# Layer 1's banded attention in blocks of 64 keys and 96 queries, on 64x64 tiles of TensorE

## The chip, the core and the metric

The kernel runs on one core of a Trainium2 chip. The metric is the device time of one execution in microseconds (us); lower is better. PE is the matmul engine (TensorE), PEld its weight loads, DVE the vector engine, ACT the scalar engine, POOL the general one, SP the queue that issues most DMAs. SBUF is the on-chip memory that all engines read; PSUM holds matmul results, in eight banks of 512 f32 numbers for each of 128 partitions.

## What is computed

x has 128 rows of 256 positions with 256 channels. Two layers follow each other, each `x + attention(groupnorm(x))`, with attention among the 256 positions of one row. Layer 0 has eight heads of 32 channels, a bias from pairs and a gate. Layer 1, which the change is about, has four heads of 64 channels and a band:

```python
q, k, v = jnp.split(x2 @ w_in.T + b_in, 3, axis=-1)      # four heads of 64
scores = jnp.einsum('bhid,bhjd->bhij', q, k) / sqrt(64)
keep = jnp.abs(i - j) <= 16                               # 256 queries i, 256 keys j
attn = softmax(jnp.where(keep, scores, -inf), axis=-1)
out = jnp.einsum('bhij,bhjd->bhid', attn, v)
y = out @ w_out.T + b_out
```

All data and all matmuls are f32.

## The kernel before, in words

An early stage transposes weights, takes statistics of x and computes layer 0's pair bias. A loop over rows does layer 0 and stores x1 to memory, a second one does layer 1, and a last block, entered only if a softmax sum was out of bounds, repeats all with a shifted softmax.

Layer 1's loop runs over s, the row. Each row has these parts, on PE unless another engine is named:

- `piece(s, 0)`: four transposes into `px` (L222), and two DVE operations (L227) that normalise it into `xn`.
- `piece(s, 1)` and `piece(s, 2)`: the q and k projections `p1q`, `p1k` (L239), channel by position; ACT adds the bias and writes `1q`, `1k` (L430), two operations each.
- `piece(s, 3)`: the v projection `p1v` (L250), position by channel in two halves of 128 positions; DVE adds the bias and writes `1v` (L435).
- `scores(s)`: for each head and each of two blocks of 128 keys one matmul over the 144 queries that the band can reach (L445), with keys as output partitions and 64 channels as rows, into one bank `1sim` per head. ACT takes Exp of each into `1ex` (L453), POOL multiplies by the 0/1 mask `seen` into `1p` (L455).
- `attend(s)`: v times p into `1av`, and a matrix of ones times p into `1zs`, the softmax sums (L472), each 64 output partitions by 144 queries. ACT copies the sums to `1z` and adds them up (L479); DVE takes the reciprocal `1rz` (L481), multiplies into `1at` (L483), and keeps the smallest sum in `zmin` (L485).
- `finish(s)`: the output projection `1po` (L250); DVE adds its bias into `1o` (L495), POOL adds x1 (L496), and every four rows SP stores them (L498).

`px`, `p1q`, `p1k`, `p1v` and `1po` share two PSUM banks, the pool `ps_proj` (tag `proj`); `1sim` has four banks, and the pool `ps_av` two, one for `1av` and one for `1zs`. Each of the five keeps its bank until the engine that reads it is done. The loop is written as:

```python
for s in range(S + 1):
    if s < S: scores(s)
    piece(s + 1, 1); piece(s + 1, 2); piece(s + 1, 3)
    piece(s + 2, 0)
    finish(s - 1)
    if s < S: attend(s)
```

The order on each engine is not exactly the written one. Tile, the framework, orders the instructions when the kernel is built: among those whose inputs and buffers it reckons ready, the one written first goes first. On the chip each engine then works in that fixed order, and waits on semaphores.

Of the kernel before, what the change touches and what calls it, by code (L numbers as in the profile page):

```python
# [9 lines left out]
F32 = mybir.dt.float32  # L10
# [5 lines left out]
P = 128  # L16
# [4 lines left out]
H0, D0 = 8, 32  # L21
H1, D1 = 4, 64
BAND = 16
KQ = P + BAND
QLO = (0, R - KQ)
NEG = -3.0e38
EPS = 1e-5
Z_LOW, Z_HIGH = 1e-12, 1e15
# [3 lines left out]
def conv_preact_kernel(  # L32
# [19 lines left out]
    dram = ctx.enter_context(tc.tile_pool(name="dram", bufs=1, space=bass.MemoryType.DRAM))  # L52
    ps_proj = ctx.enter_context(tc.tile_pool(name="ps_proj", bufs=2, space=PSUM))
    ps_sim = ctx.enter_context(tc.tile_pool(name="ps_sim", bufs=4, space=PSUM))
    ps_av = ctx.enter_context(tc.tile_pool(name="ps_av", bufs=1, space=PSUM))

    def proj_bank(name):
        return ps_proj.tile([P, 2, R], F32, tag="proj", name=name)

    def sim_bank(name):  # L60
        return ps_sim.tile([P, 2, R], F32, tag="sim", name=name)
# [19 lines left out]
    bqk = const.tile([P, 4], F32, name="bqk")  # L81
    with nc.allow_non_contiguous_dma(reason="512 biases, once"):
        nc.scalar.dma_start(out=bqk, in_=b_in[0 : 2 * C].rearrange("(t p) -> p t", p=P))
    bv = const.tile([P, C], F32, name="bv")
    nc.scalar.dma_start(out=bv, in_=b_in[2 * C : 3 * C].partition_broadcast(P))
    bo = const.tile([P, C], F32, name="bo")
    nc.scalar.dma_start(out=bo, in_=b_out.partition_broadcast(P))

# [4 lines left out]
        )  # L93


    seen = const.tile([P, 2, KQ], F32, name="seen")
    nc.gpsimd.memset(seen, 1.0)
    for kt in range(2):
        d = kt * P - QLO[kt]
        keep(seen[:, kt, :], KQ, 0.0, BAND + d, 1, -1)  # L100
        keep(seen[:, kt, :], KQ, 0.0, BAND - d, -1, 1)

    w_in_t = const.tile([P, 2, 3 * C], F32, name="w_in_t")
    w_out_t = const.tile([P, 2, C], F32, name="w_out_t")
# [49 lines left out]


    with ExitStack() as early:
        xs_pool = early.enter_context(tc.tile_pool(name="xs", bufs=2))
        pr_pool = early.enter_context(tc.tile_pool(name="pr", bufs=2))
        st_pool = early.enter_context(tc.tile_pool(name="st", bufs=1))
# [106 lines left out]
    with ExitStack() as lay:  # L266
        st1 = lay.enter_context(tc.tile_pool(name="st1", bufs=1))
        stats1 = st1.tile([P, G, S // SG, 6], F32, name="stats1")
        with ExitStack() as lay0:
            big = lay0.enter_context(tc.tile_pool(name="big0", bufs=2))  # L270
            row = lay0.enter_context(tc.tile_pool(name="row0", bufs=2))
            att = lay0.enter_context(tc.tile_pool(name="att0", bufs=2))
# [129 lines left out]
        mean1, rstd1 = group_columns(st1, stats1, 1)  # L402


    with ExitStack() as lay:
        big = lay.enter_context(tc.tile_pool(name="big1", bufs=3))
        row = lay.enter_context(tc.tile_pool(name="row1", bufs=2))
        att = lay.enter_context(tc.tile_pool(name="att1", bufs=2))
        st, hd, xgs, outs = {}, {}, {}, {}

        def load(g):
            if g * XG < S:
                xg = big.tile([P, XG, 2, C], F32, tag="xg", name=f"yg{g}")
                nc.sync.dma_start(out=xg, in_=rows(x1, g * XG, XG))
                xgs[g] = xg

        def piece(s, n):
            if s >= S:
                return
            if n == 0:  # L420
                if s % XG == 0:
                    load(s // XG + 1)
                st[s] = {"xn": normalized(row, xgs[s // XG][:, s % XG], mean1, rstd1, f"1_{s}")}
            elif n in (1, 2):
                w = "qk"[n - 1]
                ps = by_channel(w_in_t, (n - 1) * C, st[s]["xn"], f"p1{w}{s}")
                a = row.tile([P, 2, R], F32, tag=w, name=f"1{w}{s}")
                for half in range(2):
                    b = bqk[:, 2 * (n - 1) + half : 2 * (n - 1) + half + 1]
                    nc.scalar.activation(a[:, half, :], ps[:, half, :], AF.Identity, bias=b)  # L430
                st[s][w] = a
            else:
                ps = by_token(st[s]["xn"], w_in_t, 2 * C, f"p1v{s}")
                v = row.tile([P, 2, C], F32, tag="v", name=f"1v{s}")
                nc.vector.tensor_tensor(v, ps, bv.unsqueeze(1).to_broadcast([P, 2, C]), ALU.add)  # L435
                st[s]["v"] = v

        def scores(s):
            q, k = st[s]["q"], st[s]["k"]
            sims = [sim_bank(f"1sim{s}_{h}") for h in range(H1)]  # L440
            for half in range(2):
                for kt in range(2):
                    for j in range(2):
                        p0 = D1 * j
                        nc.tensor.matmul(  # L445
                            sims[2 * half + j][:, kt, 0:KQ],
                            lhsT=k[p0 : p0 + D1, half, kt * P : (kt + 1) * P],
                            rhs=q[p0 : p0 + D1, half, QLO[kt] : QLO[kt] + KQ],
                            start=True, stop=True,
                        )  # L450
            ex = att.tile([P, H1, 2, KQ], F32, tag="ex", name=f"1ex{s}")
            for h in range(H1):
                nc.scalar.activation(ex[:, h], sims[h][:, :, 0:KQ], AF.Exp, scale=1.0 / math.sqrt(D1))  # L453
            p = att.tile([P, H1, 2 * KQ], F32, tag="p", name=f"1p{s}")
            nc.gpsimd.tensor_tensor(  # L455
                p, ex.rearrange("p h k q -> p h (k q)"),
                seen.rearrange("p k q -> p (k q)").unsqueeze(1).to_broadcast([P, H1, 2 * KQ]), ALU.mult,
            )
            hd[s] = p

        def attend(s):
            p, v = hd.pop(s), st[s]["v"]
            av = ps_av.tile([P, 2, R], F32, tag="avz", name=f"1av{s}")
            zs = ps_av.tile([P, 2, R], F32, tag="bv0", name=f"1zs{s}")
            for to in (av, zs):
                for half in range(2):
                    for kt in range(2):
                        for j in range(2):
                            h = 2 * half + j
                            w = v[:, kt, h * D1 : (h + 1) * D1] if to is av else ones  # L470

                            nc.tensor.matmul(  # L472
                                to[D1 * j : D1 * (j + 1), half, QLO[kt] : QLO[kt] + KQ],
                                lhsT=w, rhs=p[:, h, kt * KQ : (kt + 1) * KQ],
                                start=(kt == 0), stop=(kt == 1), skip_group_check=True,
                            )
            z = att.tile([P, 2, R], F32, tag="z", name=f"1z{s}")
            n = 2 * S + s
            nc.scalar.activation(z, zs, AF.Identity, accum_out=zsum[:, n : n + 1])  # L479
            rz = att.tile([P, 2, R], F32, tag="rz", name=f"1rz{s}")  # L480
            nc.vector.reciprocal(rz, z)  # L481
            at = row.tile([P, 2, R], F32, tag="at", name=f"1at{s}")
            nc.vector.tensor_tensor(at, av, rz, ALU.mult)  # L483
            st[s]["at"] = at
            nc.vector.tensor_reduce(zmin[:, n : n + 1], z, axis=AX.XY, op=ALU.min)  # L485

        def finish(s):
            if s < 0:
                return
            po = by_token(st[s]["at"], w_out_t, 0, f"1po{s}")  # L490
            g, k = divmod(s, XG)
            if k == 0:
                outs[g] = big.tile([P, XG, 2, C], F32, tag="o", name=f"1o{g}", bufs=2)
            o = outs[g]
            nc.vector.tensor_tensor(o[:, k], po, bo.unsqueeze(1).to_broadcast([P, 2, C]), ALU.add)  # L495
            nc.gpsimd.tensor_tensor(o[:, k], o[:, k], xgs[g][:, k], ALU.add)  # L496
            if k == XG - 1:
                nc.sync.dma_start(out=rows(out[0], g * XG, XG), in_=o)  # L498
                outs.pop(g)
            st.pop(s)  # L500

        load(0)
        for n in range(4):
            piece(0, n)
        piece(1, 0)
        for s in range(S + 1):
            if s < S:
                scores(s)
            piece(s + 1, 1)
            piece(s + 1, 2)  # L510
            piece(s + 1, 3)
            piece(s + 2, 0)
            finish(s - 1)
            if s < S:
                attend(s)


    low = const.tile([P, 1], F32, name="low")
# [10 lines left out]
    sure = nc.values_load(n_fine[0:1, 0:1])  # L529
    with tc.If(sure < P):  # L530
        with ExitStack() as lay:
            one = lay.enter_context(tc.tile_pool(name="one2", bufs=1))
            two = lay.enter_context(tc.tile_pool(name="two2", bufs=2))
            mask = one.tile([P, 2, R], F32, name="mask2")
            nc.gpsimd.memset(mask, 0.0)
            for t in range(2):
                keep(mask[:, t, :], R, NEG, BAND + t * P, 1, -1)
                keep(mask[:, t, :], R, NEG, BAND - t * P, -1, 1)
            stats2 = one.tile([P, G, NX, 6], F32, name="stats2")

            def shifted(sim, t2, name):
# [55 lines left out]
            def again(layer, s, src, dst, mean, rstd):  # L597
# [16 lines left out]
                if layer == 0:  # L614
                    nc.vector.tensor_copy(v, ps)
                else:
                    nc.vector.tensor_tensor(v, ps, bv.unsqueeze(1).to_broadcast([P, 2, C]), ALU.add)
                at = two.tile([P, 2, R], F32, tag="at2", name=f"at2_{layer}")
                attention(layer, a["q"], a["k"], v, at)
                if layer == 0:  # L620
# [45 lines left out]
```

## Time and profile before

| what | value |
|---|---|
| median of 3 runs | 3971.83 us (3971.67 to 3971.9) |
| the profiled execution | 3971.9 us, span 3970.1 us |
| PE busy | 3877.4 us, 98% of the span |
| DVE busy | 2457.1 us, 62% |
| ACT busy | 1487.1 us, 37% |
| POOL busy | 501.2 us, 13% |
| mean granted PE clock | 0.951 |

The span runs from the first instruction to the last. Busy shares are averages over the early stage (cold clock, DMA), layer 0 (to about 2425 us) and layer 1 (from about 2480 us), so what a change in layer 1 is worth has to be read from that stretch. In the timeline a line gives the start, the time taken, the engine, the source line, the operation, output and inputs, the shape, and the number of instructions merged into it; square brackets hold the idle time of the engine before it and what ended that.

### The profile page before, as it was taken

The numbers are of one execution on the slowest core, as the hardware profiler recorded it, in microseconds if no ns is written. First come the engines' busy times: TensorE is split into PE (matmuls) and PEld (weight loads), VectorE is DVE, ScalarE is ACT, GpSimd is POOL, SyncE is SP. The second block draws the span as 40 slices with busy tenths as digits, with TensorE's granted clock in tenths as the row PEclk, the third lists the DMA queues.
The fourth block names the chain that finished last, engine by engine and source line by source line (L and its number), as shares of the span: only waits on it lengthen the run. The fifth ranks groups of instructions, "written<-read, shape, count | busy, mean of one in ns | idle before, by whom it ended". The sixth has DMA issues, their size and how long they took to land. (4 is left out here: it accounts for less than half of the span.)

```text
span 3970.1 us, 75105 instructions
## 1 busy us (share of the span) xinstructions
PE 3877.4 (98%) x32294; PEld 3057.5 (77%) x32294; DVE 2457.1 (62%) x4181; ACT 1487.1 (37%) x3485; POOL 501.2 (13%) x270
## 2 busy tenths in 40 slices
PE   7999999999999999999999997999999999999998
PEld 7998777777777777777777774788888888888887
DVE  5402677767776777677766777456556555555655
ACT  2223444444444444444444442333333333333332
POOL 0000000000000000000000000233333333333333
PEclk6556999999999999999999998999999999999999
DMA  9631011101110111001110100111111111111111
GB/s 360 217 106 54 12 44 33 44 12 44 33 44 12 44 35 42 26 30 44 33 41 15 44 23 22 54 43 43 53 55 43 43 43 43 60 48 43 43 43 33
DMA packets 153826, 208.83 MB, mean 53 GB/s; under 512 B 2960, under 2 KB 135824, under 8 KB 152464
## 3 DMA queue, kind: packets, MB, share of 16 engines
q1 hardware_dynamic: 150656, 201.34, 15.8%
q8 instruction: 256, 4.19, 0.4%
q10 hardware_dynamic: 2832, 2.63, 0.2%
q14 instruction: 82, 0.67, 0.1%
HBM read 136.85 MB, written 67.11 MB: 51 GB/s over the span
## 5 line engine op out<-in xcount | busy, mean ns | idle before, releaser
L455 POOL TENSOR_TENSOR 1p<-1ex,seen 128x1152 f32<-128x1152 f32 x128 | 336.0, 2625 | 2758.9 <-ACT 1ex L453 2758.9
L481 DVE RECIPROCAL 1rz<-1z 128x512 f32<-128x512 f32 x128 | 429.2, 3353 | 246.9 <-ACT 1z L479 246.9
L318 ACT ACTIVATE ex<-sim 128x512 f32<-128x512 f32 x1024 | 528.7, 602 | 129.0 <-PE sim L311 129.0
L360 DVE RECIPROCAL d<-d 128x256 f32<-128x256 f32 x256 | 445.9, 1742 | 0.0
L356 DVE TENSOR_TENSOR t<-bv,z 128x256 f32<-128x256 f32 x256 | 108.1, 422 | 460.2 <-ACT z L354 460.2
L354 ACT ACTIVATE z<-avz 128x256 f32<-128x256 f32 x256 | 98.3, 384 | 750.4 <-PE avz L349 739.2
L479 ACT ACTIVATE 1z<-1zs 128x512 f32<-128x512 f32 x128 | 76.4, 597 | 729.0 <-issue 719.8
L321 DVE TENSOR_TENSOR both<-ex 128x512 f32<-128x512 f32 x512 | 329.1, 683 | 2.9 <-ACT ex L318 2.9
L311 PE MATMUL sim<-q,k 32*128 32x256 f32 x4096 | 293.3, 400 | 0.0
L336 PE MATMUL avz<-ex,v 128*32 128x256 f32 x4096 | 275.6, 386 | 10.5 <-DVE t L357 10.5
L343 PE MATMUL bv<-bias_sb,v 128*32 128x256 f32 x4096 | 269.6, 379 | 1.1 <-DVE t L356 1.1
L311 PEld LDWEIGHTS sim<-q,k 32*128 32x128 f32 x4096 | 184.9, 184 | 110.5 <-issue 104.9
L227 DVE TENSOR_SCALAR xn<-px,mean,rstd 128x256 f32<-128x256 f32 x512 | 253.8, 537 | 23.8 <-PE px L222 21.3
L250 PE MATMUL 1po<-w_out_t,1at 128*128 128x256 f32 x1024 | 256.9, 394 | 0.8 <-DVE 1at L483 0.8
L239 PE MATMUL p1q<-xn,w_in_t 128*128 128x256 f32 x1024 | 257.0, 394 | 0.6 <-DVE xn L227 0.6
L239 PE MATMUL pq<-xn,qkv_sb 128*128 128x256 f32 x1024 | 256.7, 394 | 0.8 <-DVE xn L227 0.7
L250 PE MATMUL pv<-qkv_sb,xn 128*128 128x256 f32 x1024 | 255.1, 392 | 0.0
L250 PE MATMUL po<-out_sb,at 128*128 128x256 f32 x1024 | 247.5, 382 | 6.5 <-DVE at L363 4.9
L496 POOL TENSOR_TENSOR 1o<-1o,yg 128x512 f32<-128x512 f32 x128 | 162.9, 1273 | 701.8 <-DVE 1o L495 699.2
L239 PE MATMUL p1k<-xn,w_in_t 128*128 128x256 f32 x1024 | 242.4, 380 | 0.0
L239 PE MATMUL pg<-xn,gate_sb 128*128 128x256 f32 x1024 | 241.9, 379 | 0.0
L250 PE MATMUL p1v<-w_in_t,xn 128*128 128x256 f32 x1024 | 241.9, 379 | 0.0
(91 smaller groups left out, 6314.6 us busy)
## 6 DMA issues: line engine op xcount, KB each, us to landing
xs<-in_x_dram SPq DMA_DIRECT2D x8, 4096.0 KB, 22.1
xg<-in_x_dram SPq DMA_DIRECT2D x32, 1024.0 KB, 7.5
x<-o SPq DMA_DIRECT2D x16, 2048.0 KB, 8.4
yg<-x SPq DMA_DIRECT2D x32, 1024.0 KB, 8.1
out_dram<-1o SPq DMA_DIRECT2D x32, 1024.0 KB, 5.3
qkv_sb<-in_L_conv_qkv_proj_dram ACTq DMA_DIRECT2D x1, 768.0 KB, 13.7
w_nat<-in_L_conv_w_in_dram ACTq DMA_DIRECT2D x1, 768.0 KB, 8.0
gate_sb<-in_L_conv_gate_proj_dram ACTq DMA_DIRECT2D x1, 256.0 KB, 14.0
```

The costliest lines, as they stand in the source:

```text
L227: nc.vector.tensor_scalar(xn[:, half, :], px[:, half, :], mean[:, half : half + 1], rstd[:, half : half + 1], op0=ALU.subtract, op1=ALU.mult,)
L239: nc.tensor.matmul(ps[:, m, :], lhsT=w[:, kt, col + m * P : col + (m + 1) * P], rhs=xn[:, kt, :], start=(kt == 0), stop=(kt == 1),)
L250: nc.tensor.matmul(ps[:, t, :], lhsT=a[:, kt, t * P : (t + 1) * P], rhs=w[:, kt, col : col + C], start=(kt == 0), stop=(kt == 1),)
L311: nc.tensor.matmul(sims[j][:, kt, :], lhsT=k[p0 : p0 + D0, half, kt * P : (kt + 1) * P], rhs=q[p0 : p0 + D0, half, :], start=True, stop=True,)
L318: nc.scalar.activation(ex[:, j], sims[j], AF.Exp, scale=1.0 / math.sqrt(D0))
L321: nc.vector.tensor_tensor(both[:, j : j + 2], ex[:, j : j + 2, 0, :], ex[:, j : j + 2, 1, :], ALU.add)
L336: nc.tensor.matmul(avz[ps, 0, :], lhsT=v[:, kt, ch], rhs=ex[:, j, kt, :], start=(kt == 0), stop=(kt == 1),)
L343: nc.tensor.matmul(bv0[ps, :], lhsT=v[:, kt, ch], rhs=bias_sb[:, kt, 4 * half + j, :], start=(kt == 0), stop=(kt == 1),)
L360: nc.vector.reciprocal(d, d)
L455: nc.gpsimd.tensor_tensor(p, ex.rearrange("p h k q -> p h (k q)"), seen.rearrange("p k q -> p (k q)").unsqueeze(1).to_broadcast([P, H1, 2 ...
L481: nc.vector.reciprocal(rz, z)
L496: nc.gpsimd.tensor_tensor(o[:, k], o[:, k], xgs[g][:, k], ALU.add)
```

## The change

Layer 1's keys go in four blocks of 64, each with a window of 96 queries. TensorE is used as four tiles of 64 rows by 64 columns: in `scores` the row half is the head within a pair and the output half is the pair; in `attend` the row half is the pair and the output half the head within it. For this v is laid out with its partitions holding 64 keys twice, once for each pair of heads, and it is made by 16 matmuls of 128 rows by 64 columns. The mask, and v's bias, follow the new layout. `1av` and `1zs` become one tile `avz` of two banks, so `ps_av` is opened anew in each stage. `attend` skips the window's columns that the band cannot reach (`QIN`). The loop's order changes: `attend` now handles the row before, directly after `scores`, `finish` the row before that, and v's projection comes last. The number of `proj` banks stays at two.

```diff
-KQ = P + BAND
-QLO = (0, R - KQ)
+KB = 64
+WQ = KB + 2 * BAND
+QLO = tuple(min(max(0, KB * b - BAND), R - WQ) for b in range(R // KB))
+QIN = (slice(0, KB + BAND), slice(0, WQ), slice(0, WQ), slice(BAND, WQ))
...
-    bv = const.tile([P, C], F32, name="bv")
-    nc.scalar.dma_start(out=bv, in_=b_in[2 * C : 3 * C].partition_broadcast(P))
+    bv = const.tile([P, P], F32, name="bv")
+    for half in range(2):
+        nc.scalar.dma_start(
+            out=bv[KB * half : KB * (half + 1), :],
+            in_=b_in[2 * C + P * half : 2 * C + P * (half + 1)].partition_broadcast(KB),
+        )
...
-    seen = const.tile([P, 2, KQ], F32, name="seen")
+    seen = const.tile([P, R // KB, WQ], F32, name="seen")
+    seen_high = const.tile([P, R // KB, WQ], F32, name="seen_high")
+    for part, first in ((seen, 0), (seen_high, -KB)):
+        nc.gpsimd.memset(part, 1.0)
+        for b in range(R // KB):
...
+    nc.gpsimd.tensor_copy(seen[KB:P], seen_high[KB:P])
...
-                ps = by_token(st[s]["xn"], w_in_t, 2 * C, f"p1v{s}")
-                v = row.tile([P, 2, C], F32, tag="v", name=f"1v{s}")
-                nc.vector.tensor_tensor(v, ps, bv.unsqueeze(1).to_broadcast([P, 2, C]), ALU.add)
+                xn = st[s]["xn"]
+                ps = proj_bank(f"p1v{s}").rearrange("p a (b c) -> p (a b) c", c=P)
+                for b in range(R // KB):
+                    for kt in range(2):
+                        for half in range(2):
+                            nc.tensor.matmul(
+                                ps[KB * half : KB * (half + 1), b, :],
+                                lhsT=xn[:, kt, KB * b : KB * (b + 1)],
+                                rhs=w_in_t[:, kt, 2 * C + P * half : 2 * C + P * (half + 1)],
+                                start=(kt == 0), stop=(kt == 1),
+                            )
+                v = row.tile([P, R // KB, P], F32, tag="v", name=f"1v{s}")
+                nc.vector.tensor_tensor(v, ps, bv.unsqueeze(1).to_broadcast([P, R // KB, P]), ALU.add)
...
+            for b in range(R // KB):
+                for half in range(2):
                     for j in range(2):
                         p0 = D1 * j
                         nc.tensor.matmul(
-                            sims[2 * half + j][:, kt, 0:KQ],
-                            lhsT=k[p0 : p0 + D1, half, kt * P : (kt + 1) * P],
-                            rhs=q[p0 : p0 + D1, half, QLO[kt] : QLO[kt] + KQ],
+                            sims[j][KB * half : KB * (half + 1), b, :],
+                            lhsT=k[p0 : p0 + D1, half, KB * b : KB * (b + 1)],
+                            rhs=q[p0 : p0 + D1, half, QLO[b] : QLO[b] + WQ],
                             start=True, stop=True,
                         )
...
+            for j in range(2):
+                nc.scalar.activation(ex[:, j], sims[j], AF.Exp, scale=1.0 / math.sqrt(D1))
...
-            av = ps_av.tile([P, 2, R], F32, tag="avz", name=f"1av{s}")
-            zs = ps_av.tile([P, 2, R], F32, tag="bv0", name=f"1zs{s}")
+            avz = ps_av.tile([P, 2, 2, R], F32, tag="avz", name=f"1avz{s}")
+            for what in range(2):
+                for b in range(R // KB):
+                    for half in range(2):
                         for j in range(2):
+                            keys, cols = slice(KB * half, KB * (half + 1)), slice(D1 * j, D1 * (j + 1))
+                            q0 = QLO[b]
 
                             nc.tensor.matmul(
+                                avz[cols, half, what, q0 + QIN[b].start : q0 + QIN[b].stop],
+                                lhsT=v[keys, b, cols] if what == 0 else ones[keys, :],
+                                rhs=p[keys, j, b, QIN[b]],
+                                start=(what == 0 and b == 0), stop=(what == 1 and b == R // KB - 1),
+                                skip_group_check=True,
                             )
...
-        for s in range(S + 1):
+        for s in range(S + 2):
             if s < S:
                 scores(s)
+            if s <= S:
+                attend(s - 1)
+            finish(s - 2)
             piece(s + 1, 1)
             piece(s + 1, 2)
+            piece(s + 2, 0)
             piece(s + 1, 3)
-            piece(s + 2, 0)
-            finish(s - 1)
-            if s < S:
-                attend(s)
```

More of the change, by code (lines that the diff above doesn't have):

```diff
@@ L54, in conv_preact_kernel, with av_pool @@
     ps_sim = ctx.enter_context(tc.tile_pool(name="ps_sim", bufs=4, space=PSUM))
-    ps_av = ctx.enter_context(tc.tile_pool(name="ps_av", bufs=1, space=PSUM))
+    def av_pool(scope, name):
+        return scope.enter_context(tc.tile_pool(name=name, bufs=1, space=PSUM))
     def proj_bank(name):
@@ L93, in keep @@
         )
-    seen = const.tile([P, 2, KQ], F32, name="seen")
[L97 to L101, printed above, removed]
+    seen = const.tile([P, R // KB, WQ], F32, name="seen")
[3 more added lines that the diff above has]
+        for b in range(R // KB):
+            d = first + KB * b - QLO[b]
+            keep(part[:, b, :], WQ, 0.0, BAND + d, 1, -1)
+            keep(part[:, b, :], WQ, 0.0, BAND - d, -1, 1)
+    nc.gpsimd.tensor_copy(seen[KB:P], seen_high[KB:P])
     w_in_t = const.tile([P, 2, 3 * C], F32, name="w_in_t")
@@ L156, in conv_preact_kernel @@
     with ExitStack() as early:
+        ps_av = av_pool(early, "ps_av_early")
         xs_pool = early.enter_context(tc.tile_pool(name="xs", bufs=2))
@@ L269, in conv_preact_kernel @@
         with ExitStack() as lay0:
+            ps_av = av_pool(lay0, "ps_av0")
             big = lay0.enter_context(tc.tile_pool(name="big0", bufs=2))
@@ L405, in conv_preact_kernel @@
     with ExitStack() as lay:
+        ps_av = av_pool(lay, "ps_av1")
         big = lay.enter_context(tc.tile_pool(name="big1", bufs=3))
@@ L439, in scores @@
             q, k = st[s]["q"], st[s]["k"]
-            sims = [sim_bank(f"1sim{s}_{h}") for h in range(H1)]
-            for half in range(2):
-                for kt in range(2):
+            sims = [
+                sim_bank(f"1sim{s}_{j}").rearrange("p a b -> p (a b)")[:, 0 : 4 * WQ]
+                .rearrange("p (b q) -> p b q", q=WQ)
+                for j in range(2)
+            ]
+            for b in range(R // KB):
+                for half in range(2):
                     for j in range(2):
@@ L445, in scores @@
                         nc.tensor.matmul(
-                            sims[2 * half + j][:, kt, 0:KQ],
-                            lhsT=k[p0 : p0 + D1, half, kt * P : (kt + 1) * P],
-                            rhs=q[p0 : p0 + D1, half, QLO[kt] : QLO[kt] + KQ],
+                            sims[j][KB * half : KB * (half + 1), b, :],
+                            lhsT=k[p0 : p0 + D1, half, KB * b : KB * (b + 1)],
+                            rhs=q[p0 : p0 + D1, half, QLO[b] : QLO[b] + WQ],
                             start=True, stop=True,
                         )
[L451 to L454, printed above, removed]
+            ex = att.tile([P, 2, 4, WQ], F32, tag="ex", name=f"1ex{s}")
+            for j in range(2):
+                nc.scalar.activation(ex[:, j], sims[j], AF.Exp, scale=1.0 / math.sqrt(D1))
+            p = att.tile([P, 2, 4, WQ], F32, tag="p", name=f"1p{s}")
             nc.gpsimd.tensor_tensor(
-                p, ex.rearrange("p h k q -> p h (k q)"),
-                seen.rearrange("p k q -> p (k q)").unsqueeze(1).to_broadcast([P, H1, 2 * KQ]), ALU.mult,
+                p.rearrange("p j b q -> p j (b q)"), ex.rearrange("p j b q -> p j (b q)"),
+                seen.rearrange("p b q -> p (b q)").unsqueeze(1).to_broadcast([P, 2, 4 * WQ]), ALU.mult,
             )
@@ L461, in attend @@
         def attend(s):
+            if s < 0:
+                return
             p, v = hd.pop(s), st[s]["v"]
-            av = ps_av.tile([P, 2, R], F32, tag="avz", name=f"1av{s}")
-            zs = ps_av.tile([P, 2, R], F32, tag="bv0", name=f"1zs{s}")
-            for to in (av, zs):
-                for half in range(2):
-                    for kt in range(2):
+            avz = ps_av.tile([P, 2, 2, R], F32, tag="avz", name=f"1avz{s}")
+            for what in range(2):
+                for b in range(R // KB):
+                    for half in range(2):
                         for j in range(2):
-                            h = 2 * half + j
-                            w = v[:, kt, h * D1 : (h + 1) * D1] if to is av else ones
+                            keys, cols = slice(KB * half, KB * (half + 1)), slice(D1 * j, D1 * (j + 1))
+                            q0 = QLO[b]
                             nc.tensor.matmul(
-                                to[D1 * j : D1 * (j + 1), half, QLO[kt] : QLO[kt] + KQ],
-                                lhsT=w, rhs=p[:, h, kt * KQ : (kt + 1) * KQ],
-                                start=(kt == 0), stop=(kt == 1), skip_group_check=True,
+                                avz[cols, half, what, q0 + QIN[b].start : q0 + QIN[b].stop],
[3 more added lines that the diff above has]
+                                skip_group_check=True,
                             )
@@ L478, in attend @@
             n = 2 * S + s
-            nc.scalar.activation(z, zs, AF.Identity, accum_out=zsum[:, n : n + 1])
+            nc.scalar.activation(z, avz[:, :, 1, :], AF.Identity, accum_out=zsum[:, n : n + 1])
             rz = att.tile([P, 2, R], F32, tag="rz", name=f"1rz{s}")
@@ L482, in attend @@
             at = row.tile([P, 2, R], F32, tag="at", name=f"1at{s}")
-            nc.vector.tensor_tensor(at, av, rz, ALU.mult)
+            nc.vector.tensor_tensor(at, avz[:, :, 0, :], rz, ALU.mult)
             st[s]["at"] = at
@@ L531, in conv_preact_kernel @@
         with ExitStack() as lay:
+            ps_av = av_pool(lay, "ps_av2")
             one = lay.enter_context(tc.tile_pool(name="one2", bufs=1))
@@ L538, in conv_preact_kernel @@
                 keep(mask[:, t, :], R, NEG, BAND - t * P, -1, 1)
+            bv_row = one.tile([P, 2, P], F32, name="bv_row")
+            nc.sync.dma_start(
+                out=bv_row.rearrange("p a b -> p (a b)"), in_=b_in[2 * C : 3 * C].partition_broadcast(P)
+            )
             stats2 = one.tile([P, G, NX, 6], F32, name="stats2")
@@ L616, in again @@
                 else:
-                    nc.vector.tensor_tensor(v, ps, bv.unsqueeze(1).to_broadcast([P, 2, C]), ALU.add)
+                    for half in range(2):
+                        nc.vector.tensor_tensor(
+                            v[:, :, P * half : P * (half + 1)], ps[:, :, P * half : P * (half + 1)],
+                            bv_row[:, half].unsqueeze(1).to_broadcast([P, 2, P]), ALU.add,
+                        )
                 at = two.tile([P, 2, R], F32, tag="at2", name=f"at2_{layer}")
```

## The prediction

> **What bounds the kernel now.** I start with the page: busy shares and the slices of the span.
>
> ```profile
> span 3970.1 us, 75105 instructions
> PE 3877.4 (98%) x32294; PEld 3057.5 (77%) x32294; DVE 2457.1 (62%) x4181; ACT 1487.1 (37%) x3485; POOL 501.2 (13%) x270
> ...
> PE   7999999999999999999999997999999999999998
> ```
>
> PE is busy throughout. But the change is in layer 1 alone, from slice 25 on, so I next read the busy times by stretch:
>
> ```profile
> 3000.00:3500.00 500.00, 500.00 (x3670) 418.36 (x3670) 297.81 (x308) 161.60 (x439) 170.22 (x87) 1.00 0.16 47
> ```
>
> In the steady part of layer 1 PE has work in 500 of 500 us at full clock, DVE in 298. The layer is bound by PE, if its order has no hole. The timeline of PE alone shows one row of 128 (start, duration, instruction, count):
>
> ```profile
> 3010.63 1.25 PE L445 MATMUL 1sim<-1q,1k 64*128 64x144 f32 x16
> 3011.81 1.99 PE L239 MATMUL p1q<-xn,w_in_t 128*128 128x256 f32 x8
> 3013.64 1.89 PE L239 MATMUL p1k<-xn,w_in_t 128*128 128x256 f32 x8
> 3015.37 1.89 PE L250 MATMUL p1v<-w_in_t,xn 128*128 128x256 f32 x8
> 3017.10 0.60 PE L222 MATMUL px<-ident,yg 128*128 128x128 f32 x4
> 3017.63 0.70 PE L472 MATMUL 1av<-1p,1v 128*64 128x144 f32 x6
> 3018.26 1.99 PE L250 MATMUL 1po<-w_out_t,1at 128*128 128x256 f32 x8
> ...
> 3020.86 1.26 PE L472 MATMUL 1zs<-1p,ones 128*64 128x144 f32 x15
> 3022.05 0.52 PE L445 MATMUL 1sim<-1q,1k 64*128 64x144 f32 x4
> ```
>
> Scores to scores is 22.05 - 3010.63 less 3000, **11.42 us a row**. Each f32 matmul leaves two records (four of p1q make x8). From the trace's single records: a 256-column one starts 216 ns after the one before, a 128-column px 109, so a record costs about N/1.2 + 2.5 ns. The 64-wide ones of L445 and L472 start in pairs 7 ns apart, a pair every 122 ns (144/1.2 + 2.5): two tiles work at once. Layer 0's 32-wide tiles go in fours, 216 ns a four. A change of tile shape costs extra: L472 to L445 and then on to p1q 0.19 and 0.20 us, px to 1av 0.14, 1av to 1po 0.20, back 0.14; 0.87 us a row.
>
> Second thing to see: six records of 1av stand ahead of 1po, though `attend` is written after `finish`. The order is Tile's, made when the kernel is built: 1po was waiting for one of the two `proj` banks (p1v's, still being read by DVE), and ready work was put in. The other engines in the same row, from the timeline of all engines:
>
> ```profile
> 3010.79 0.60 ACT L479 ACTIVATE 1z<-1zs 128x512 f32<-128x512 f32 x1 [5.73 <-issue]
> ...
> 3011.51 3.35 DVE L481 RECIPROCAL 1rz<-1z 128x512 f32<-128x512 f32 x1 [1.94 <-ACT 1z L479]
> ...
> 3013.91 0.84 ACT L430 ACTIVATE 1q<-p1q,bqk 128x256 f32<-128x256 f32 x2 [1.10 <-PE p1q L239]
> ...
> 3020.35 0.69 DVE L495 TENSOR_TENSOR 1o<-1po,bo 128x512 f32<-128x512 f32 x1 [1.46 <-issue]
> ```
>
> The 3.35 us reciprocal blocks DVE while PE does p1q and p1k, whose banks ACT empties; 1o, which empties 1po's bank, is far from it. Today nothing waits for the reciprocal.
>
> **What the Trainium skill says.** "TensorEngine Tiling (Array Packing)", Key Properties: tiles of different position run loads and matmuls in parallel, and a change of tiling mode drains the engine. The trace agrees on both, with the pairs and the 0.14 to 0.20 us above. "TensorE: Matmul & The Clock Gate", LDWEIGHTS: a load costs its columns over 1.2 ns. The trace agrees in the slope: 137 ns for 64 columns, 190 for 128. So a 64-column load (53 ns) fits behind an 80-column record (69 ns). Same page, Part 3: 16 tiles gained 10.6x; no run here shows rows and columns split together.
>
> **The change part by part**, per row, PE first.
> - Scores: 16 matmuls of 96 columns in fours: 32 records, 8 groups x 82.5 ns = 0.66 us. Now 16 records, 8 pairs x 122.5 = 0.98.
> - Attend: 32 matmuls of 80 or 96 columns: 64 records, 16 groups, half 69.2 ns and half 82.5: 1.21. Now 18 groups (split before 1po) x 122.5 = 2.20.
> - v: 16 matmuls of 128 columns and two tiles: 32 records, 16 pairs x 109 = 1.75. Now 8 x 216 = 1.73.
> - po, q, k: 24 x 216 = 5.18; px 4 x 109 = 0.44. Unchanged.
> - Tile shapes: attend follows scores in one shape, so three changes (attend to po 0.20, px to v 0.14, v to scores 0.14) = 0.48. No row shows a 64x64 change; between 0 and 0.20 each I take the like of those seen.
>
> Sum 9.72 us, that is **1.70 us a row under 11.42, or 217 us over 128 rows if nothing waits**.
>
> Other engines: Exp goes from four of 288 columns to two of 384; between the rows for 288 (415 ns) and layer 0's 512 (602) that is 495 each, about 0.9 us for 1.32. POOL's mask product shrinks from 1152 to 768 columns, 2.63 to 1.75, and is wanted only a row later. z, reciprocal, at, o, v keep 512 columns. More masks on POOL and one more DMA issue on ACT's queue come once, 2300 us ahead of use, beside a first stage that loads data: nothing; if that cover were gone, a few us. `avz` is one tile of two banks: the next attend waits for at, done some 4 us before. `finish` comes a row later than it did: SP's store of four rows goes out a row later, and its load of yg, four rows (over 40 us) ahead of use and 8.1 us to land by the page, still finds its buffer freed a row before. Nothing for both.
>
> **The moved steps.** Now T = 0 at the first scores. Attend ends at 1.87, po runs 2.07 to 3.80, q 3.80 to 5.53. Meanwhile z starts 0.25 after attend (as at 3010.79) and takes 0.79 with its accumulator read; the reciprocal starts at 2.94. po's bank is free for DVE only at 4.05, so its add sits **behind the reciprocal**, zmin and at: 2.94 + 3.27 + 0.55 + 0.61 (issue steps of the trace) = 7.37, done 8.06. k wants a bank at 5.53. The other bank is q's: ACT begins 0.26 after q and takes 0.84, and with 0.12 to PE k starts at 6.75. **Stall 1.22.** Behind k on PE stand px, v and the next scores, and for k itself waits ACT's 1k. k ends 8.48; px takes po's bank, to 8.92; v waits for k's bank, 8.48 + 1.22 = 9.70, of which 0.14 is the shape change: **stall 0.64**. v to 11.45, change 0.14: the row takes 11.59. If Tile puts some of the next attend into the px-v hole, as it did before 1po, about 0.1 comes off. q of the next row and po find their banks empty. So 11.46 to 11.59; I take 11.54, +0.12 x 128 = 15 us. The end gains one more trip round the loop with a single row in it; by the gaps of today's last two rows some 3 us. 3971.9 + 18 = **3990 us**. The profiled execution took 3971.9 (span 3970.1 and 1.8 around it), the median is 3971.83: the same. The order that Tile makes can put v after the first score, or an attend between, a shape change or two and 0.1 to 0.3 us each way: 11.25 to 11.95, **3950 to 4040 us** for this case.
>
> **Rivals.**
> 1. Faster: the hole isn't there. If Tile lets po's add go before the reciprocal (done 4.74), k starts at 5.53; v still waits for k, 7.26 + 1.22 = 8.48, and the row takes 10.1 to 10.4: 3971.9 - 128 x 1.0 to 1.3 = 3805 to 3844. It decides if z becomes ready later than po's result, that is over 1.1 us later than I have it, or if PE gets other ready work. For it: PE's sum and DVE's 7 us a row both fit in 9.7. Against: DVE takes work as it becomes ready (zmin runs ahead of at in the trace, written after it).
> 2. Slower, banks by turn: if `proj` banks go strictly round, k waits for po's bank, 8.06 + 0.1; px then takes q's, v waits for k: about 13.0, +200 us, 4175. The trace of before gives the same order either way, so it cannot exclude it.
> 3. The tiles don't do what is said: rows share a bus or the queue can't issue 96 loads and matmuls so fast (before shows 8 per 216 ns, the change asks 8 per 69). With two at a time 1.87 us become 3.74: row 13.4, +255 us, 4227. At before's 8 per 216 it would be worse, 24 groups x 0.216 = 5.2. Against: within a four, starts are 7 ns apart with a load each.
>
> **How the numbers follow.** A measurement here tells 0.2%, 8 us, from no change. The base case gets 0.62: its row must exceed 11.47 to be slower, and I split it 0.38 slower, 0.14 same, 0.10 faster. Rival 1 gets 0.20, rivals 2 and 3 together 0.18. Faster 0.30, same 0.14, slower 0.56. The range holds the base case, rival 1's upper part and the milder ends of 2 and 3: 3815 to 4130.
>
> **What would show it.** Right: scores at two starts per 82 ns or four together; PE idle over 1 us a row ahead of p1k, ended by ACT's 1q L430; DVE's 1o directly behind 1at; a smaller hole ahead of p1v. Wrong: PE at 500 of 500 us again with a shorter row (rival 1); p1k released by DVE's 1o (rival 2); records of L445's and L472's successors 7 ns apart only in twos (rival 3).

## The result, and the profile after

The changed kernel takes **3996.62 us** (median of 4 runs, 3996.24 to 3996.9) against 3971.86 in the runs beside it: ratio 1.0062, 95% interval 1.0045 to 1.008. It is slower by 25 us, where 18 were forecast. The page of the profile after:

```profile
span 3995.1 us, 93174 instructions
PE 3776.7 (95%) x41510; PEld 2978.1 (75%) x41510; DVE 2456.2 (61%) x4181; ACT 1429.8 (36%) x3229; POOL 399.7 (10%) x284
```

PE is busy 101 us less than before, ACT 57, POOL 101, and the span is 25 us longer. The page's slices don't tell why: a slice is some 100 us, and a hole in each row leaves PE at 9 tenths. The busy times of the same stretch as before show it:

```profile
3000.00:3500.00 500.00, 457.24 (x6711) 384.39 (x6710) 291.54 (x303) 139.36 (x344) 132.32 (x86) 1.00 0.16 48
```

PE was busy 500 of 500 us and is now busy 457. One row of layer 1, PE's timeline from q's projection to the next:

```profile
3019.80 1.89 PE L252 MATMUL p1q<-xn,w_in_t 128*128 128x256 f32 x8
3022.68 1.99 PE L252 MATMUL p1k<-xn,w_in_t 128*128 128x256 f32 x8 [0.99 <-ACT 1q L447]
3024.51 0.60 PE L235 MATMUL px<-ident,yg 128*128 128x128 f32 x4
3025.04 0.35 PE L505 MATMUL 1avz<-1p,1v 64*64 64x80 f32 x2
3025.30 0.38 PE L476 MATMUL 1sim<-1q,1k 64*64 64x96 f32 x4
3025.66 1.97 PE L455 MATMUL p1v<-w_in_t,xn 128*64 128x128 f32 x32
...
3029.58 1.99 PE L263 MATMUL 1po<-w_out_t,1at 128*128 128x256 f32 x8
3031.41 1.89 PE L252 MATMUL p1q<-xn,w_in_t 128*128 128x256 f32 x8
```

q to q is **11.61 us**, 11.42 before. The hole (time in which PE has nothing to do) that was forecast stands ahead of p1k, in square brackets, and ACT's `1q` ends it. Ahead of p1v Tile put in one matmul of attend and two of the scores. DVE and ACT in that row, from the timeline of all engines:

```profile
3018.87 3.35 DVE L516 RECIPROCAL 1rz<-1z 128x512 f32<-128x512 f32 x1 [2.12 <-ACT 1z L514]
3021.78 0.84 ACT L447 ACTIVATE 1q<-p1q,bqk 128x256 f32<-128x256 f32 x2 [2.95 <-PE p1q L252]
3022.14 0.63 DVE L520 TENSOR_REDUCE zmin<-1z 128x1 f32<-128x512 f32 x1
3022.68 0.67 DVE L518 TENSOR_TENSOR 1at<-1avz,1rz 128x512 f32<-128x512 f32 x1
3023.28 0.68 DVE L530 TENSOR_TENSOR 1o<-1po,bo 128x512 f32<-128x512 f32 x1
```

PE goes on from po to q at 3019.80, but the add that empties po's bank, `1o`, runs only at 3023.28, behind reciprocal, zmin and at. Until then only one bank is left for q and k, and k starts 0.06 us after ACT is done with q.

### The profile page after: what moved, and what is told of

The parts are those of the page before. It is cut to its first block, busy times and chain, and to the rows that moved or that the text cites. A ratio compares the mean times of both kernels' runs of the same rounds, so it can differ in the third digit from the quotient of the medians.

```text
span 3995.1 us, 93174 instructions
## 1 busy us (share of the span) xinstructions
PE 3776.7 (95%) x41510; PEld 2978.1 (75%) x41510; DVE 2456.2 (61%) x4181; ACT 1429.8 (36%) x3229; POOL 399.7 (10%) x284
## 5 line engine op out<-in xcount | busy, mean ns | idle before, releaser
L486 POOL TENSOR_TENSOR 1p<-1ex,seen 128x768 f32<-128x768 f32 x128 | 232.0, 1813 | 3038.4 <-ACT 1ex L484 3038.4
L252 PE MATMUL p1k<-xn,w_in_t 128*128 128x256 f32 x1024 | 255.8, 393 | 123.8 <-ACT 1q L447 123.8
L252 PEld LDWEIGHTS p1k<-xn,w_in_t 128*128 128x128 f32 x1024 | 185.0, 190 | 194.3 <-ACT 1q L447 174.0
L455 PE MATMUL p1v<-w_in_t,xn 128*64 128x128 f32 x4096 | 251.9, 276 | 0.0
L252 PE MATMUL p1q<-xn,w_in_t 128*128 128x256 f32 x1024 | 244.0, 381 | 0.6 <-DVE xn L240 0.6
L447 ACT ACTIVATE 1q<-p1q,bqk 128x256 f32<-128x256 f32 x256 | 107.5, 471 | 382.1 <-PE p1q L252 382.1
L484 ACT ACTIVATE 1ex<-1sim 128x384 f32<-128x384 f32 x256 | 111.6, 489 | 370.6 <-PE 1sim L476 370.6
```

Of the source, the lines that this page charges most:

```text
L252: nc.tensor.matmul(ps[:, m, :], lhsT=w[:, kt, col + m * P : col + (m + 1) * P], rhs=xn[:, kt, :], start=(kt == 0), stop=(kt == 1),)
L455: nc.tensor.matmul(ps[KB * half : KB * (half + 1), b, :], lhsT=xn[:, kt, KB * b : KB * (b + 1)], rhs=w_in_t[:, kt, 2 * C + P * half : 2 * ...
L486: nc.gpsimd.tensor_tensor(p.rearrange("p j b q -> p j (b q)"), ex.rearrange("p j b q -> p j (b q)"), seen.rearrange("p b q -> p (b q)").un ...
```

## Experiments

Each starts from the changed kernel unless it says otherwise, and was timed against the kernel before on the same chip. Besides the theory, two explanations stand in the expectations: rival U, that two banks and ACT's time after q cost this wait whatever DVE does; rival V, that the small tiles save less than was worked out.

**1. finish behind k's projection.**

```diff
-            finish(s - 2)
             piece(s + 1, 1)
             piece(s + 1, 2)
+            finish(s - 2)
             piece(s + 2, 0)
```

> The changed kernel (11.61 us a row) with finish(s-2) written after k's projection instead of before q's. Theory (po's bank is held because its DVE add stands behind the reciprocal, so k waits for q's bank): q and k find empty banks, po follows in q's bank, its add comes about when the reciprocal chain ends anyway; only v waits a little for po's bank. A row of 10.1 to 10.2, 3972 - 128 x 1.25 = about 3810 us. Rival U (two banks and ACT's 1.1 us after q always cost this wait, whatever DVE does): k still waits for a bank, 3990 to 4000. Rival V (the small tiles save less than worked out, the rest is shape changes and split groups): no better than 3900.

3794.79 us, ratio 0.9553 (0.9537 to 0.9569). Lines of all engines:

```profile
3019.63 3.35 DVE L516 RECIPROCAL 1rz<-1z 128x512 f32<-128x512 f32 x1 [1.97 <-ACT 1z L514]
3020.56 1.89 PE L252 MATMUL p1k<-xn,w_in_t 128*128 128x256 f32 x8
3020.82 0.84 ACT L447 ACTIVATE 1q<-p1q,bqk 128x256 f32<-128x256 f32 x2 [1.22 <-PE p1q L252]
```

k now starts at 3020.56, before ACT has touched q: both banks were empty. The same instructions in another order take 202 us less than in the change. That speaks against both rivals. It is also 15 us less than worked out: a row takes 10.0 us, just under the 10.1 to 10.2 expected.

**2. Four proj banks, two score banks** in layer 1, the loop as in the change. PSUM's eight banks are shared out anew for each stage, and the other stages keep two and four; of the edit, the line for layer 1:

```diff
...
+        banks(lay, "1", n_proj=4, n_sim=2)
         ps_av = av_pool(lay, "ps_av1")
...
```

> The changed kernel with layer 1's PSUM shared out anew: four proj banks and two score banks instead of two and four; the order of the loop stays. Theory: no projection waits for a bank, k follows q at once and v follows px; the row is PE's own sum, 9.72 us, 3972 - 128 x 1.70 = about 3755 us, with PE at 500 of 500 us. Rival U: the same, since the wait is one for banks in both. Rival V: over 3800, PE busy without a hole but with longer groups or shape changes. If two score banks are too few, a new wait of the scores for Exp appears.

**3762.49 us**, ratio 0.9473 (0.9457 to 0.9489), the fastest of the kernels here that compute everything. A row in PE's timeline:

```profile
3011.75 0.89 PE L481 MATMUL 1sim<-1q,1k 64*64 64x96 f32 x32
3012.46 0.79 PE L510 MATMUL 1avz<-1p,1v 64*64 64x80 f32 x32
3013.07 0.79 PE L510 MATMUL 1avz<-1p,ones 64*64 64x80 f32 x32
3013.79 1.99 PE L266 MATMUL 1po<-w_out_t,1at 128*128 128x256 f32 x8
3015.62 1.89 PE L255 MATMUL p1q<-xn,w_in_t 128*128 128x256 f32 x8
3017.34 1.89 PE L255 MATMUL p1k<-xn,w_in_t 128*128 128x256 f32 x8
3019.07 0.60 PE L238 MATMUL px<-ident,yg 128*128 128x128 f32 x4
3019.60 1.97 PE L460 MATMUL p1v<-w_in_t,xn 128*64 128x128 f32 x32
3021.50 0.89 PE L481 MATMUL 1sim<-1q,1k 64*64 64x96 f32 x32
```

There is no hole and no piece put in; a row is 9.75 us. Scores and attend take 2.04 us from the first score to po, with the change of shape; the prediction had 2.07. PE's sum in the prediction holds, so rival V falls. On rival U this run says nothing, as the expectation states.

**3. The kernel before with the new order alone.**

> The kernel before with only the loop's new order (attend of the row before right after scores, finish of the row before that, v last). Theory: the order alone brings the holes ahead of k and v; without faster tiles the row grows from 11.42 to 11.7 to 12.2 us, as Tile fills part of the holes with pieces of attend at the price of shape changes: 4010 to 4070 us. Rival V (the order is harmless, the tiles are what disappoints): 3965 to 3980.

4096.98 us, ratio 1.0315 (1.0298 to 1.0332): slower, as expected, but 27 us beyond the upper end. The row is 12.43 us. PE's timeline of it, in part:

```profile
3011.69 0.60 PE L222 MATMUL px<-ident,yg 128*128 128x128 f32 x4
3012.22 0.46 PE L472 MATMUL 1av<-1p,1v 128*64 128x144 f32 x2
3012.61 0.51 PE L445 MATMUL 1sim<-1q,1k 64*128 64x144 f32 x2
3013.05 1.99 PE L250 MATMUL p1v<-w_in_t,xn 128*128 128x256 f32 x8
...
3021.17 1.19 PE L472 MATMUL 1zs<-1p,ones 128*64 128x144 f32 x14
```

Here PE looks full, 499.93 of 500 us from 3000 on, but the holes are only filled. Tile puts seven matmuls of zs (14 records) into the one ahead of k, and one of av and one of the scores into the one ahead of v. Each filled hole brings two or three changes of tile shape: the row has eight where the kernel before has five. The theory expected such filling and set its price too low. px to v takes 1.36 us for 0.44 us of px and two small matmuls. So the new order costs 1.0 us a row with the old tiles; with it, the new tiles win back 0.8.

**4. Without the reciprocal** (`at` is avz times z).

> The changed kernel without the reciprocal of layer 1: the attention is multiplied by the sums instead of divided by them; all else stays. Theory: po's bank is free at about 4.7 us of the row, k follows q at once, v still waits for k's bank; a row of 10.3 to 10.4, about 3835 us. Rival U (ACT's reading of q alone makes k wait): unchanged, 3990 to 4000. DVE falls from 7 to 3.7 us a row, which was not the bound.

3831.98 us, ratio 0.9647 (0.9631 to 0.9663), as worked out. PE's lines, from the timeline of all engines:

```profile
3016.99 1.89 PE L252 MATMUL p1q<-xn,w_in_t 128*128 128x256 f32 x8
3018.72 1.89 PE L252 MATMUL p1k<-xn,w_in_t 128*128 128x256 f32 x8
```

k starts 1.73 us after q, with no hole: `1o`, which starts at 3017.27 and takes 0.68, has emptied po's bank by then. Only v still waits. DVE was never the busiest engine: in the change its reciprocal costs time by standing ahead of 1o. There are two banks as before, and ACT reads q as before, yet k doesn't wait: rival U falls.

**5. The new tiles in the old order.**

> The changed kernel's tiles, masks, layout of v and PSUM, with the loop's order of the kernel before (q, k, v, px, finish of the row before, attend of this row last). Theory: the reciprocal falls again beside q and k, whose banks ACT empties; po waits for v's bank as before, and part of attend is put in ahead of it at the price of shape changes. From PE's sum 9.72 with two more shape changes (0.34) and a wait of about 0.5 ahead of po: 10.5 to 10.6 a row, about 3862 us. If the tiles were worth nothing without the new order: 3950 or more.

3848.31 us, ratio 0.969 (0.9674 to 0.9706), 14 us better than worked out (a row of 10.39). The tiles alone are worth 123 us. The order that came with them costs 148: it takes the 123 back and 25 more. With the old tiles (experiment 3) the same order cost 125.

**6. Reciprocal written after finish**, so that 1o goes ahead of zmin and at. The three are moved out of `attend` into `divide`; of the edit, the line in the loop:

```diff
...
             finish(s - 2)
+            divide(s - 1)
             piece(s + 1, 1)
...
```

> The changed kernel with the reciprocal, at and zmin written after finish, so that po's add goes before zmin and at on DVE, directly behind the reciprocal (Tile's order still has the reciprocal first, since its input is ready earlier). Theory: the reciprocal alone holds the bank long enough; po's bank is free at about 7.0 us of the row instead of 8.06, q's still earlier (6.75), so k waits as long as it did: 3985 to 3997 us. If zmin and at ahead of the add were what costs: about 0.6 us a row less, 3920.

3998.01 us, ratio 1.0066 (1.0049 to 1.0083): no different from the change, and 1 us above the range expected. The timeline of all engines, in part:

```profile
3018.94 3.35 DVE L522 RECIPROCAL 1rz<-1z 128x512 f32<-128x512 f32 x1 [2.11 <-ACT 1z L514]
...
3021.85 0.84 ACT L447 ACTIVATE 1q<-p1q,bqk 128x256 f32<-128x256 f32 x2 [2.95 <-PE p1q L252]
3022.21 0.63 DVE L536 TENSOR_TENSOR 1o<-1po,bo 128x512 f32<-128x512 f32 x1
```

Counted from q, the add is 1.1 us earlier than in the change, but it ends at 3022.84, still after ACT is done with q (3022.69). The reciprocal ahead of it is enough to make k wait; with it there, zmin and at add nothing to the time. Writing the reciprocal after `finish` didn't get 1o ahead of it either.

**7. Three proj banks and three score banks.**

> The changed kernel with three proj banks and three score banks in layer 1, order as in the change. Theory: k takes the third bank at once; the next short place is v, which waits for po's bank until its add, behind the reciprocal, is done at about 8.1 us of the row: a row of 10.0 to 10.1, about 3797 us, between two banks (3997) and four (3762). If any third bank removes all waits: 3762.

3831.09 us, ratio 0.9647 (0.9631 to 0.9664): between two and four banks, but 34 us more than worked out. k waits for nothing. Between px and v, PE's lines and that of 1o, from the timeline of all engines:

```profile
3016.55 0.60 PE L238 MATMUL px<-ident,yg 128*128 128x128 f32 x4
3016.57 0.68 DVE L535 TENSOR_TENSOR 1o<-1po,bo 128x512 f32<-128x512 f32 x1
...
3017.08 0.35 PE L510 MATMUL 1avz<-1p,1v 64*64 64x80 f32 x2
...
3017.34 0.38 PE L481 MATMUL 1sim<-1q,1k 64*64 64x96 f32 x2
3017.64 1.97 PE L460 MATMUL p1v<-w_in_t,xn 128*64 128x128 f32 x32
```

`1o` was done at 3017.25, so po's bank was free for v 0.39 us before v started. v stood behind two matmuls that Tile had put in, and one more shape change. They cost more than the wait that they were to fill: px to v is 1.09 us, with four banks 0.53. Each of them works alone and takes 0.26 to 0.30 us up to the next start, the second with a change of shape; a full group of four matmuls of the scores takes 0.165, two records of 82 ns. And they give nothing back: from v to the next po it is 3.93 us in both, though here two matmuls fewer are left for that stretch. This is the term that the expectation left out. That filling is the whole of the 34 us is read from the trace and was not tried by itself.

**8. Four banks and no reciprocal.**

> Four proj banks as before, and without layer 1's reciprocal (the attention is multiplied by the sums instead of divided by them). Theory: with no wait for a bank the reciprocal lies wholly beside PE's work, so taking it away changes nothing: 3755 to 3766 us, while with two banks it was worth 165 us. If DVE still bound something: lower.

3753.14 us, ratio 0.9451 (0.9435 to 0.9466), 9 us less than with four banks, and 2 us below the range expected. The rows are the same: q's starts of rows 20 to 110 are 9.746 us apart in both traces. Most of the difference is the end: from q's last record to the end of the span it is 31.5 us with the reciprocal, 23.5 without. There PE stands idle for 3.55 and 1.93 us until `1at`, behind the reciprocal, is done. So in the loop the reciprocal costs nothing once the banks suffice, where with two banks taking it away was worth 165 us, all but 9 of them ahead of the last q.

## Why the prediction was right

- **PE's sum, 9.72 us.** 9.75 with four banks. Fours at 82 ns show in single records of the trace after (a four of attend starts at 3028.41, the next at 3028.49). The 64x64 shape changes, taken to be like the others, are so: with four banks 0.15 us from v to scores and 0.21 from attend to po.
- **The hole ahead of k, 1.22.** q to k is 2.88 us where it is 1.73 without a wait: 1.15, since PE started 0.06 us after ACT was done and not 0.12. (The profile calls 0.99 of it idle, because it counts q's last record to its modelled end; the sign in the prediction was "over 1 us".) The order on DVE and the releaser were as forecast, and experiments 1, 2 and 4 each take the hole away by another way.
- **The hole ahead of v, 0.64 beyond the shape change.** px to v is 1.15 us, with four banks 0.53: 0.62.
- **A row of 11.54 as the value taken.** 11.62 as the mean of rows 20 to 110. Two terms that lengthen it were missed or mis-sized. The matmul after a hole takes 0.10 us more, as after a shape change (1.83 from k to px, 1.73 elsewhere), which the walk left out. And the pieces put in ahead of v were to save about 0.1, of which the value taken counts half, and save nothing (v to po is 3.92 us, with four banks 3.93): 9.75 + 1.15 + 0.10 + 0.62 = 11.62.
- **The end, +3 us.** 0.21 x 127 = 27 us for the rows against 25.0 for the spans, so the first rows and the end together come out about 2 us shorter, not 3 longer. The end alone, from q's last start, is 34.1 us where it was 33.8.
- **How near the number came.** The mechanism was right for the reasons given, but a forecast of 18 us against 25 measured is in part luck: the two terms above make up some 19 us over 128 rows, as much as the whole forecast, and the shorter hole and the end took back most of it.
- **Rivals.** The faster one, 3805 to 3844, had the row right for a kernel in which k doesn't wait (experiment 4; experiment 1, with another order, is shorter still), but not its condition: Tile keeps the reciprocal first even where it is written after `finish` (experiment 6). Banks by turn: k was released by ACT's `1q` and so took q's bank. Tiles that run two at a time: refuted by the 2.04 us of experiment 2.

## What to carry over

When PE's work gets shorter, ask which buffer each step needs next and which engine empties it, in that engine's own order; a long instruction on an engine that is some 60% busy can hold a PSUM bank and stop one that was 100% busy. A split of PSUM that fits one order of steps need not fit the next: here two banks moved from the scores to the projections turned 25 us lost into 209 us won. And matmuls that a framework slips into a hole aren't free when they change the tile shape; a PE that is 100% busy can still be filling holes.

## Not expected of the hardware

The granted clock that the profile gives for the early stage differs between executions of the same work: 0.54 over the first 350 us in the change, 1.00 with four banks. Yet PE is busy 323.57 and 323.58 us there, and in both the records of the transposes `pz` start 213 ns apart, where those of `px`, of the same shape, start 109 ns apart in layer 1. So PE went through that stage at about half its later rate in both, and the 1.00 doesn't tell what the matmuls ran at: with four banks the trace holds no record of the clock before 360 us, and the figure takes such time as full speed.
